# A gated graph network followed by graph attention, planned at build time: the order of the first layers, the last pair's second layer, and the plan's offsets

## The chip, the core and the metric

The kernel runs on one core of a Trainium2 chip. The engines named below are TensorE (PE; its weight loads are listed apart, as PEld), VectorE (DVE), ScalarE (ACT), GpSimd (POOL) and SyncE (SP), which issues the transfers. The time is the device time of one execution in microseconds, from its start to its end. One of the executions is recorded by the hardware profiler, and all rows of this document come from such a record.

## The reference

The input is 64 graphs of 256 nodes with 256 features, and an adjacency matrix for each with about 3% of its entries set. Two blocks follow one another, each with a layer norm, a relu and a residual. The first is three layers of a gated recurrent unit (GRU) over messages of the neighbours, the second one layer of graph attention.

```python
A = (adj != 0)
h = relu(layernorm(x))
for i in range(3):
    aggr = A.T @ (h @ weight[i])
    gi, gh = aggr @ w_ih.T + b_ih, h @ w_hh.T + b_hh
    r, z = sigmoid(i_r + h_r), sigmoid(i_z + h_z)
    n = tanh(i_n + r * h_n)
    h = (1 - z) * n + z * h
x = x + h
h = relu(layernorm(x)) @ W.T
e = leaky_relu(h @ a_left + (h @ a_right).T, 0.2)
x = x + softmax(where(adj == 0, -1e9, e)) @ h
```

`weight` differs from layer to layer, while `w_ih`, `w_hh` and the biases are shared.

## The kernel before

**Tiles.** Two graphs make a pair, and there are 32 pairs. A tile is 128 partitions by 512 elements: 128 features by the 2 x 256 nodes of a pair (the state `hT`, one tile for each of two blocks of features, 0 and 1), or 128 nodes by features in the other orientation. All tiles come from fixed classes: 28 `full` (f32), 22 `round` (TensorE's rounded f32), 40 `half` (16 bit), 8 PSUM banks, and a few more.

**Precision.** Matmuls take split operands. `split16` makes of a value its rounded head (name ending in `0`, on ScalarE), its remainder in 16 bits (`1`, on VectorE) and its whole in 16 bits (`d`). A gate is then one pass over heads (weights `fac_*`) and two over 16-bit parts (weights `low_*`), all accumulated in one bank (`gate`, L671, its matmuls at L668). The setup multiplies `weight[i]` by `w_ih` once (`G`, L595), so a layer computes its messages as `A.T @ h` and goes straight to the gates. `limbs` (L652) makes the head and the remainder, `hi` and `lo`, that the propagation takes.

**A layer of a pair** (in `pair`, L746) consists of: the splits of the state (`h0`, `h1`), the propagation `prop` on TensorE (L805), the splits of its result (`g0`, `g1`, from the bank), and for each block of features four gates: `r`, `nh` (own state, scaled at L690), `ni`, `z`. Behind them stand the sigmoid and tanh on ScalarE (L823, L833, L836) and five passes on VectorE: `u` L828, `u add` L831, `d sub` L840, `d mul` L842, `d add` L844. The new state is then turned back to the orientation that the next propagation needs. Pairs 1 to 30 do this by a transposing DMA (`dma_turn`, L700), gathers (L705) and a joining copy on ScalarE (`join`, L713). The first and the last pair do it on TensorE (`back`, L871). The last pair's last layer runs graph by graph, with 256 columns for each gate, and with its own back-transposes (L856). Two or more pairs are in work at a time.

**The attention** of a pair: norm and relu (L728 to L741), dot products on VectorE (L899), `right` (over DRAM, or by a transpose on TensorE in the last pair, L920), leaky relu (L925), mask (L928), max (L930), exponentials (L936; L1010 in the last pair), the transpose of the probabilities (by DMA, in the last pair on TensorE, L1018), `mix` (L965, L973, L1026) and `project` (L984, L995, L1034), the output (L1000, L1037) and its store (L1003). The last two pairs mix and project in plain f32 (L973, L995, L1026, L1034), the others with split operands.

**What sets the order.** Nothing is scheduled on the chip: each engine runs its queue in order. The queues are filled at build time by `Plan`, a list scheduler. Each operation has an engine, a time for which it occupies it and a time after which its result is there, all written as constants. Priorities are due times carried back along the dependences, less an offset from the table `LEAD`. That table is keyed by the operation's name, with a prefix for the first pair, the last (`last `) and the one before it (`late `); pairs without a prefix share one set of offsets, so the order repeats from pair to pair. Two things lie outside the priorities: `in_turn` makes the groups of gates (one for each layer of each pair) follow each other by a turn number, and `stage` holds a layer's entry back until an earlier group has begun. The turn number of layer i of pair p is 3p + 2i. So TensorE's gates run pair 0 layer 0, pair 0 layer 1, pair 1 layer 0, pair 0 layer 2, pair 1 layer 1, pair 2 layer 0 and so on: from there on one layer of another pair lies between two layers of a pair, but layers 0 and 1 of pair 0 are neighbours, and so are layers 1 and 2 of pair 31.

**The start.** `rows` (biases and attention vectors, L492 to L494) and the weights (`w load`, L511) are loaded, turned on TensorE (L522, L569), copied (L529) and split (`factor`, L545 to L552).

## Time and profile before

| | us |
|---|---|
| three runs | 1955.44, 1958.47, 1960.41 |
| median | 1958.47 |
| profiled execution | 1956.43 |
| its span, first to last instruction | 1954.6 |
| first TensorE instruction, from the span's start | 5.5 |

| work | busy us | instructions |
|---|---|---|
| matmuls of the gates (three groups of L668 by weights `low_hh`, `low`, `fac_hh`) | 621.7, 620.5, 433.4 | 2328, 2328, 1164 |
| joins on ScalarE, L713 | 342.5 | 304 |

A group's busy time is the sum over its instructions, its mean the time of one. TensorE's matmuls overlap in the record: the end of each is modelled and lies past the next one's start, so the spacing of two starts, not the duration, is what one costs. Idle time is shown with the instruction that ended it ("releaser"). The granted clock of TensorE is 0.998 of full speed on average; it is at half speed in a few stretches, the last ones of which begin at 1909.9 and 1940.6 us.

### The profile page before, as it was taken

The page shows a single profiled execution, that of the slowest core. Times are in us where ns is not written, and L with a number is a line of the kernel's source. Part 1 is how long each engine was busy: PE and PEld are TensorE (multiplying, and loading weights), DVE is VectorE, ACT ScalarE, POOL GpSimd, SP SyncE. Part 2 cuts the span into 40 slices and gives each one's busy share as a digit, 9 for nine tenths or more (in the row PEclk, how much of TensorE's full clock was granted, in tenths as well). Part 3 has the DMA queues.
Part 4 walks back from the last instruction along what each step waited for, and adds up shares of the span by engine and source line. Part 5 has one row for each costly group of instructions (what it writes and reads, how often), then busy time and mean ns, then how long its engine had stood idle before and what let it go on. Part 6 is the DMA issues. An engine that isn't in the chain of part 4 may idle for free.

```text
span 1954.6 us, 31416 instructions
## 1 busy us (share of the span) xinstructions
PE 1930.9 (99%) x10205; PEld 1198.8 (61%) x10205; DVE 1646.6 (84%) x3954; ACT 1609.6 (82%) x2773; POOL 199.4 (10%) x262
## 2 busy tenths in 40 slices
PE   8999999999999999999999999999999999999998
PEld 5566655666656666666656666666556566666667
DVE  7688888888898888888888888888888888898886
ACT  5578888888888888888889888888888888888875
POOL 2001011011011011111010110110110111110100
PEclk9999999999999999999999999999999999999999
DMA  4247876868776678966687766698766777666733
GB/s 123 48 78 144 137 135 123 115 122 138 141 135 121 116 130 137 143 123 119 121 138 141 135 122 117 120 142 139 127 122 113 140 136 139 123 118 121 122 76 60
DMA packets 734469, 239.43 MB, mean 122 GB/s; under 512 B 658256, under 2 KB 734304, under 8 KB 734304
## 3 DMA queue, kind: packets, MB, share of 16 engines
q1 hardware_dynamic: 734272, 237.41, 68.5%
q8 instruction: 80, 1.31, 0.3%
q14 instruction: 85, 0.70, 0.2%
q10 hardware_dynamic: 32, 0.01, 0.0%
HBM read 61.09 MB, written 16.84 MB: 40 GB/s over the span
## 4 chain that ended last, share of the span: by engine, by line
PE 82%; ACT 6%; DMA 5%; DVE 5%; issue 1%; SPq 1%; ACTq 0%; DVEq 0%
PE bank L668 66%; PE bank L805 7%; DMA full<-full 4%; PE bank L965 3%; PE bank L984 3%; ACT full L713 2%; ACT round L619 1%; SPq L705 1%; PE bank L595 1%; DVE half L625 1%; ACT half L630 1%; DVE full L828 1%; ACT round L654 1%; DVE full L1000 1%; ACT full L741 0%
## 5 line engine op out<-in xcount | busy, mean ns | idle before, releaser
L668 PE MATMUL bank<-half,low_hh 128*128 128x512 f16 (+1 forms) x2328 | 621.7, 378 | 5.3 <-DVE half L625 5.2
L668 PE MATMUL bank<-half,low 128*128 128x512 f16 (+1 forms) x2328 | 620.5, 378 | 1.2 <-DVE half L623 1.2
L668 PE MATMUL bank<-round,fac_hh 128*128 128x512 f32 (+1 forms) x1164 | 433.4, 454 | 0.0
L668 PEld LDWEIGHTS <-low_hh 128*128 128x128 f16 x2328 | 211.1, 98 | 271.5 <-issue 64.9
L713 ACT COPY full<-full 128x1024 uint16<-128x1024 uint16 x304 | 342.5, 1162 | 37.1 <-DMA full<-full 23.4
L668 PEld LDWEIGHTS <-low 128*128 128x128 f16 x2328 | 203.3, 98 | 275.4 <-issue 83.2
L668 PE MATMUL bank<-round,fac 128*128 128x512 f32 (+1 forms) x1164 | 367.1, 405 | 0.0
L668 PEld LDWEIGHTS bank<-round,fac 128*128 128x128 f32 x1164 | 217.5, 188 | 56.4
L668 PEld LDWEIGHTS bank<-round,fac_hh 128*128 128x128 f32 x1164 | 212.8, 189 | 62.9
L735 POOL TENSOR_TENSOR small<-small,nhalf 128x2 f32<-128x2 f32 x128 | 122.2, 955 | 1243.3 <-DVE small L733 1239.1
L833 ACT ACTIVATE full<-full,vec 128x512 f32<-128x512 f32 (+1 forms) x194 | 138.8, 717 | 83.3 <-DVE full L831 82.6
L836 ACT ACTIVATE full<-bank,b_rz 128x512 f32<-128x512 f32 (+1 forms) x194 | 131.3, 677 | 70.6 <-PE bank L668 68.7
L623 DVE TENSOR_TENSOR half<-bank,round 128x512 f16<-128x512 f32 x192 | 131.6, 687 | 59.8 <-ACT half L630 45.4
L625 DVE SCALAR_TENSOR_TENSOR half<-full,round 128x512 f16<-128x512 f32 x252 | 167.0, 682 | 2.4 <-ACT round L619 2.4
L655 DVE SCALAR_TENSOR_TENSOR half<-full,round 128x512 f16<-128x512 f32 x184 | 123.8, 688 | 46.4 <-ACT round L654 45.7
L690 ACT ACTIVATE bank<-bank,b_nh 128x512 f32<-128x512 f32 (+1 forms) x194 | 127.1, 655 | 40.7 <-PE bank L668 40.2
L823 ACT ACTIVATE full<-bank,b_rz 128x512 f32<-128x512 f32 (+1 forms) x194 | 131.7, 679 | 32.0 <-PE bank L668 25.9
L630 ACT ACTIVATE half<-bank 128x512 f16<-128x512 f32 x252 | 146.4, 597 | 11.7 <-PE bank L805 11.2
L619 ACT ACTIVATE round<-bank 128x512 fp32r<-128x512 f32 x252 | 146.8, 597 | 10.2 <-PE bank L805 9.2
L840 DVE TENSOR_TENSOR full<-full,full 128x512 f32<-128x512 f32 (+1 forms) x194 | 132.3, 682 | 25.9 <-ACT full L833 25.9
L619 ACT ACTIVATE round<-full 128x512 fp32r<-128x512 f32 x252 | 146.2, 629 | 2.2 <-DVE full L844 2.0
L842 DVE SCALAR_TENSOR_TENSOR full<-full,full 128x512 f32<-128x512 f32 (+1 forms) x194 | 132.1, 681 | 11.7 <-ACT full L836 10.3
(113 smaller groups left out, 2566.8 us busy)
## 6 DMA issues: line engine op xcount, KB each, us to landing
full<-full SPq DMA_DIRECT2D x484, 128.0 KB, 3.6
x<-in_x_dram SPq DMA_DIRECT2D x64, 256.0 KB, 3.1
adj<-in_adj_dram SPq DMA_DIRECT2D x64, 256.0 KB, 3.8
full<-in_x_dram SPq DMA_DIRECT2D x64, 256.0 KB, 3.7
full<-full SPq DMA_DIRECT2D x248, 64.0 KB, 3.3
out_dram<-full SPq DMA_DIRECT2D x62, 256.0 KB, 2.2
full<-line SPq DMA_DIRECT2D x62, 128.0 KB, 3.8
full<-full SPq DMA_TRANSPOSE x304, 3.4
```

What stands on the lines that cost most here:

```text
L619: act(name + " 0", A512 if bank else C512, lambda: nc.scalar.activation(v0.t, v.t, AF.Copy, scale=up), r=[(v, ALL)], w=[(v0, ONE)])
L623: rem = lambda: nc.vector.tensor_sub(v1.t, v.t, v0.t.bitcast(F32))
L625: rem = lambda: nc.vector.scalar_tensor_tensor(v1.t, v.t, up, v0.t.bitcast(F32), op0=ALU.mult, op1=ALU.subtract)
L630: act(name + " d", A512, lambda: nc.scalar.activation(vd.t, v.t, AF.Copy, scale=up), r=[(v, ALL)], w=[(vd, ONE)])
L668: return [(j, lambda start, j=j, kb=kb: nc.tensor.matmul(bank.t[:, cols], fs(j, kb), s[kb][j].t[:, cols], start=start, stop=True, skip_gro ...
L713: act(name, 1065, lambda: nc.scalar.copy(dst.t.bitcast(U16).rearrange("p (j n b) -> p j n b", j=2, b=2), src.t.bitcast(U16).rearrange(f"p ...
L805: nc.tensor.matmul(pa.t[:, ts(g, N)], b, m[:, ts(sb, N)], start=(n == 0), stop=True, skip_group_check=True)
L823: act(f"r {db}{of}", fit(575, part), lambda b=r_, k=pr, db=db, cols=cols: nc.scalar.activation(b.t[:, cols], k.t[:, cols], AF.Tanh, bias=b ...
L833: act(f"tanh {db}{of}", fit(615, part), lambda u=u, en=en, cols=cols: nc.scalar.activation(u.t[:, cols], u.t[:, cols], AF.Tanh, bias=b_i[: ...
L836: act(f"z {db}{of}", fit(575, part), lambda b=z_, k=pz, db=db, cols=cols: nc.scalar.activation(b.t[:, cols], k.t[:, cols], AF.Tanh, bias=b ...
L840: dve2(f"d sub {db}{of}", fit(V512, part), lambda u=u, d=d, cols=cols: nc.vector.tensor_sub(d.t[:, cols], d.t[:, cols], u.t[:, cols]), r=[ ...
L842: dve2(f"d mul {db}{of}", fit(V512, part), lambda d=d, b=z_, cols=cols: nc.vector.scalar_tensor_tensor(d.t[:, cols], b.t[:, cols], 1.0, d. ...
```

## The change

Four edits, and a new table of offsets.

1. The turn numbers come from a table `TURN`, in which layers 0 and 1 of pair 1 get the numbers 1 and 3. The order of the gates at the start becomes pair 0 layer 0, pair 1 layer 0, pair 0 layer 1, pair 1 layer 1, pair 0 layer 2, and goes on as before.
2. In the last pair, layer 1 runs graph by graph too (`apart` for i > 0): its gates, back-transposes and limbs. The entry of its layer 2 (splits of the state, propagation, splits of its result) runs graph by graph as well (`entry`). For this `split16` and `limbs` are rewritten to work on a part of the columns, and the gates read by parts. The pair has 320 operations in place of 272: 18 more on VectorE, 16 on ScalarE, 14 on TensorE. All other pairs have the operations they had.
3. In the plan, the result of `rows` is put at 5300 ns after its issue (3000 before), that of a weight load at 3900 (3434), with 500 ns of SyncE for each (600).
4. Pair 29 gets a prefix of its own, `pen `.
5. All offsets in `LEAD` are new, and so the order of all queues.

The remainder of the propagation's split, a subtraction before, becomes a `scalar_tensor_tensor` with a factor of 1.0.

```diff
...
-    "A": -93000, "A16": 28000, "G": -2000, "b_nh": 8000, "b_rz": -33500, "b_rz half": -33000, "back 0": -60500,
...
+    "A": -122000, "A16": -24000, "b_nh": 12000, "b_rz": -99500, "back 0": 113000, "back 0 gather": 5500,
...
+    "pen tanh 1": -40000, "pen total": -16000, "pen turn 0": 8000, "pen turn 0 gather": -9000, "pen turn 1": -16000,
...
-        plan.op("rows", "ACT", 200, 3000, load_rows, w=[(rw, ONE)])
+        plan.op("rows", "ACT", 200, 5300, load_rows, w=[(rw, ONE)])
...
-                dma("w load", 256, lambda b=b, r0=r0: nc.sync.dma_start(parts(b), view[:, r0 : r0 + 2, :]), w=[(b, ONE)])
+                plan.op("w load", "SP", 500, 3900, lambda b=b, r0=r0: nc.sync.dma_start(parts(b), view[:, r0 : r0 + 2, :]), w=[(b, ONE)])
...
-    def rounded(name, v, v0, up, bank=False):
-        act(name + " 0", A512 if bank else C512, lambda: nc.scalar.activation(v0.t, v.t, AF.Copy, scale=up), r=[(v, ALL)], w=[(v0, ONE)])
-    def remainder(name, v, v0, v1, up, dve_):
-        if up == 1.0:
-            rem = lambda: nc.vector.tensor_sub(v1.t, v.t, v0.t.bitcast(F32))
+    def split16(name, v, up, bank=False, part=None, whole=None, unit=C):
+        v0, v1, vd = whole or (Buf("round"), Buf("half"), Buf("half"))
+        cols, of = (slice(None), "") if part is None else (columns(part), " of %d" % part[0])
+        has = keys = ALL if part is None else part
+        cut = lambda ns: ns if part is None else fit(ns, part)
+        dve_ = dve if bank else dve2
+        act(f"{name} 0{of}", cut(A512 if bank else C512), lambda: nc.scalar.activation(
+            v0.t[:, cols], v.t[:, cols], AF.Copy, scale=up), r=[(v, has)], w=[(v0, keys)])
+        dve_(f"{name} 1{of}", cut(V512), lambda: nc.vector.scalar_tensor_tensor(
+            v1.t[:, cols], v.t[:, cols], up, v0.t[:, cols].bitcast(F32), op0=ALU.mult, op1=ALU.subtract), r=[(v, has), (v0, keys)], w=[(v1, keys)])
+        if bank:
+            act(f"{name} d{of}", cut(A512), lambda: nc.scalar.activation(
+                vd.t[:, cols], v.t[:, cols], AF.Copy, scale=up * unit), r=[(v, has)], w=[(vd, keys)])
         else:
-            rem = lambda: nc.vector.scalar_tensor_tensor(v1.t, v.t, up, v0.t.bitcast(F32), op0=ALU.mult, op1=ALU.subtract)
-        dve_(name + " 1", V512, rem, r=[(v, ALL), (v0, ONE)], w=[(v1, ONE)])
-    def whole_of(name, v, vd, up, bank):
-        if bank:
-            act(name + " d", A512, lambda: nc.scalar.activation(vd.t, v.t, AF.Copy, scale=up), r=[(v, ALL)], w=[(vd, ONE)])
-        else:
-            dve2(name + " d", 340, lambda: nc.vector.tensor_scalar(vd.t, v.t, up, None, op0=ALU.mult), r=[(v, ALL)], w=[(vd, ONE)])
-    def split16(name, v, up, bank=False, given=(None, None), part=None):
-        v0, v1 = given
-        vd = Buf("half")
-        if v0 is None:
-            v0 = Buf("round")
-            rounded(name, v, v0, up, bank)
-        if v1 is None:
-            v1 = Buf("half")
-            remainder(name, v, v0, v1, up, dve if bank else dve2)
-        whole_of(name, v, vd, up * (part or C), bank)
+            dve2(f"{name} d{of}", cut(340), lambda: nc.vector.tensor_scalar(
+                vd.t[:, cols], v.t[:, cols], up * unit, None, op0=ALU.mult), r=[(v, has)], w=[(vd, keys)])
         return v0, v1, vd
-    def turn16(name, src, cols, dst, place, n, **kw):
-        plan.op(name, "SP", T16, 4100, lambda: nc.sync.dma_start_transpose(
-            dst.t.bitcast(U16)[:, place].rearrange("p (c n) -> p c n", n=P), cols(src.t.bitcast(U16))), **kw)
-    def limbs(tag, v, b, c, dve_):
-        act(tag[0], C512, lambda: nc.scalar.activation(b.t, v.t, AF.Copy, scale=UP_V), r=[(v, ALL)], w=[(b, ONE)])
-        dve_(tag[1], V512, lambda: nc.vector.scalar_tensor_tensor(
-            c.t, v.t, UP_V, b.t.bitcast(F32), op0=ALU.mult, op1=ALU.subtract), r=[(v, ALL), (b, ONE)], w=[(c, ONE)])
+    def limbs(tag, v, b, c, dve_, part=None):
+        cols = slice(None) if part is None else columns(part)
+        src = lambda: v.t if part is None else v.t[:, :N]
+        keys = ALL if part is None else part
+        cut = lambda ns: ns if part is None else fit(ns, part)
+        act(tag[0], cut(C512), lambda: nc.scalar.activation(b.t[:, cols], src(), AF.Copy, scale=UP_V), r=[(v, ALL)], w=[(b, keys)])
+        dve_(tag[1], cut(V512), lambda: nc.vector.scalar_tensor_tensor(
+            c.t[:, cols], src(), UP_V, b.t[:, cols].bitcast(F32), op0=ALU.mult, op1=ALU.subtract), r=[(v, ALL), (b, keys)], w=[(c, keys)])
...
-                           r=[(s[kb][j], ALL) for _, s in ts_ for kb in range(DB) for j in range(3)] + [
+                           r=[(s[kb][j], part) for _, s in ts_ for kb in range(DB) for j in range(3)] + [
...
-        plan.prefix = {0: "first ", NPAIR - 2: "late ", NPAIR - 1: "last "}.get(p, "")
-        plan.stage = (3 * p, 2)
+        plan.prefix = {0: "first ", NPAIR - 3: "pen ", NPAIR - 2: "late ", NPAIR - 1: "last "}.get(p, "")
+        plan.stage = (TURN[p, 0], 2)
...
-            plan.stage = (3 * p + 2 * i, 1)
-            hs = [split16(f"h{db}", hT[db], UP_V, given=given[db]) for db in range(DB)]
-            given = [(None, None)] * DB
-            gs = []
-            for db in range(DB):
-                pa = Buf("bank")
-                def prop(db=db, pa=pa, hi=hi, lo=lo, first=i == 0):
-                    ops = [(hi, A), (lo, A16)]
-                    terms = [(part, a, g, sb) for part, a in (ops[::-1] if narrow[0] else ops) for g in range(G) for sb in range(NB)]
-                    for n, (part, a, g, sb) in enumerate(terms):
-                        if not first:
-                            b = part[db].t[:, ts(g * NB + sb, P)]
-                        elif part is lo:
-                            b = lo[g].t[:, ts(db * NB + sb, P)]
-                        else:
-                            b = blocks_of(part[g])[:, sb, db, :]
-                        m = a[g].t.bitcast(BF16) if part is lo else a[g].t
-                        nc.tensor.matmul(pa.t[:, ts(g, N)], b, m[:, ts(sb, N)], start=(n == 0), stop=True, skip_group_check=True)
-                pe(f"prop {db}", 4 * (PROP + PROP16), prop, r=[(b, ONE) for b in (hi + lo if i == 0 else [hi[db], lo[db]]) + A + A16], w=[(pa, ONE)], mixed=True)
-                gs.append(split16(f"g{db}", pa, 1.0, True))
+            plan.stage = (TURN[p, i], 1)
+            apart, entry = i > 0 and not far, [(0,), (1,)] if last and not far else [None]
+            triple = lambda: (Buf("round"), Buf("half"), Buf("half"))
+            hs, gs = [triple() for _ in range(DB)], [triple() for _ in range(DB)]
+            for part in entry:
+                for db in range(DB):
+                    split16(f"h{db}", hT[db], UP_V, part=part, whole=hs[db])
+            pas = [Buf("bank") for _ in range(DB)]
+            for part in entry:
+                for db in range(DB):
+                    def prop(db=db, pa=pas[db], hi=hi, lo=lo, first=i == 0, graphs=part or ALL):
+                        ops = [(hi, A), (lo, A16)]
+                        terms = [(part, a, g, sb) for part, a in (ops[::-1] if narrow[0] else ops) for g in graphs for sb in range(NB)]
+                        for n, (part, a, g, sb) in enumerate(terms):
+                            if not first:
+                                b = part[db].t[:, ts(g * NB + sb, P)]
+                            elif part is lo:
+                                b = lo[g].t[:, ts(db * NB + sb, P)]
+                            else:
+                                b = blocks_of(part[g])[:, sb, db, :]
+                            m = a[g].t.bitcast(BF16) if part is lo else a[g].t
+                            nc.tensor.matmul(pa.t[:, ts(g, N)], b, m[:, ts(sb, N)], start=(n == 0), stop=True, skip_group_check=True)
+                    of, graphs = ("", ALL) if part is None else (" of %d" % part[0], part)
+                    pe(f"prop {db}{of}", 2 * len(graphs) * (PROP + PROP16), prop, mixed=True, w=[(pas[db], graphs)],
+                       r=[(b, part or ALL) for b in (hi + lo if i == 0 else [hi[db], lo[db]])] + [(b[g], ONE) for b in (A, A16) for g in graphs])
+                    split16(f"g{db}", pas[db], 1.0, True, part=part, whole=gs[db])
...
-            tops = TOPS[3 * p + 2 * i] = []
-            apart = last and not far
+            tops = TOPS[TURN[p, i]] = []
             for part in [(0,), (1,)] if apart else [ALL]:
                 cols, of = columns(part), " of %d" % part[0] if apart else ""
                 for db in range(DB):
-                    plan.due = 1000.0 * SLOT * (3 * p + 2 * i) + (8000.0 * part[0] if apart else 0)
+                    plan.due = 1000.0 * SLOT * TURN[p, i] + (8000.0 * part[0] if apart else 0)
...
+                of = " of %d" % g
                 def back(g=g, db=db, hn=hn):
                     for k in range(NB):
                         nc.tensor.transpose(hn.t[:, ts(k, P)], hT[db].t[:, ts(g * NB + k, P)], ident)
                 pe(f"back {db} of {g}", 2 * TR, back, r=[(hT[db], (g,))], w=[(hn, ALL)])
-                dve(f"res {db} of {g}", 335, lambda g=g, db=db, b=XR[g], hn=hn: nc.vector.tensor_add(
+                if not last:
+                    limbs((f"hi {db}{of}", f"lo {db}{of}"), hn, hi[db], lo[db], dve, part=(g,))
+                    continue
+                dve(f"res {db}{of}", 335, lambda g=g, db=db, b=XR[g], hn=hn: nc.vector.tensor_add(
                     parts(b)[:, :, ts(db, P)], parts(b)[:, :, ts(db, P)], hn.t[:, :N].rearrange("p (k f) -> p k f", k=NB)),
                     r=[(hn, ALL)], w=[(XR[g], ALL)])
...
-                ps = split16(f"p{g}", pT, UP_P, part=1.0)
+                ps = split16(f"p{g}", pT, UP_P, unit=1.0)
...
     TOPS, SLOT = {}, 20
+    TURN = {(p, i): 3 * p + 2 * i for p in range(NPAIR) for i in range(L)}
+    TURN.update({(1, 0): 1, (1, 1): 3})
```

## The prediction

> **What bounds the kernel now.** I read the totals first, then TensorE's waits, then windows of the stages, then the chain of waits.
>
> ```profile
> span 1954.6 us, 31416 instructions
> PE 1930.9 (99%) x10205; PEld 1198.8 (61%) x10205; DVE 1646.6 (84%) x3954; ACT 1609.6 (82%) x2773; POOL 199.4 (10%) x262
> ```
>
> TensorE is busy 99% of the span. A reordering can only win what TensorE stands still, runs at a low clock, or spends before its first and after its last matmul. The waits show where it stands:
>
> ```profile
> PE bank L498 <- DMA rows<-in_L_gnn_b_hh_dram: 5.5, 1, 5.5
> PE bank L668 <- DVE half L625: 5.2, 10, 0.8
> PE bank L871 <- DVE full L844: 4.4, 4, 1.9
> PE bank L1018 <- ACT full L1010: 3.2, 1, 3.2
> PE bank L668 <- DVE half L623: 1.2, 2, 0.8
> PE bank L805 <- DVE half L655: 0.4, 1, 0.4
> ```
>
> Columns: us in total, times, longest. Of the 4.4 us at L871 (layer output turned back on TensorE) the timeline puts 0.21 and 1.87 us at 48.4 to 50.9 (pair 0, layer 0 to 1) and 1.41 and 0.88 us at 1906 to 1909 (pair 31, layer 1 to 2). L1018, 3.2 us, is in the last pair's attention. L625, L623 and L655 are short stalls spread over the steady part. Now the stages:
>
> ```profile
> 900.00:959.00 59.00, 59.00 (x314) 36.36 (x312) 51.12 (x124) 50.58 (x87) 6.39 (x8) 1.00 0.71 130
> ...
> 1900.00:1910.00 10.00, 7.71 (x40) 4.43 (x37) 9.58 (x33) 6.82 (x12) 1.04 (x2) 1.00 0.22 33
> 1910.00:1920.00 10.00, 9.99 (x75) 8.47 (x75) 6.50 (x13) 7.04 (x18) 0.00 (x0) 0.83 0.40 74
> 1920.00:1930.00 10.00, 9.98 (x89) 8.94 (x87) 6.69 (x19) 6.51 (x17) 0.00 (x0) 1.00 0.75 107
> 1930.00:1955.00 25.00, 17.82 (x96) 15.50 (x96) 13.51 (x50) 11.40 (x29) 1.38 (x2) 0.92 0.13 43
> ```
>
> Columns: busy us of PE, PEld, DVE, ACT, POOL, then granted clock. A steady pair has TensorE full; the end does not, and from 1910 to 1920 the clock is 0.83. A pair without a stall has a length that the chain of waits gives, by one recurring gate:
>
> ```profile
> 857.97 14.70 PE bank L668 x66
> ...
> 916.96 14.70 PE bank L668 x66
> ...
> 975.94 14.70 PE bank L668 x66
> ...
> 1036.71 14.70 PE bank L668 x66
> ```
>
> These starts lie 58.99, 58.98 and 60.77 us apart: a pair costs 58.985 us, and 1.79 us were lost in the last. From 264.69 to 1749.13 lie 25 pairs in 1484.4 us, 9.8 us over 25 x 58.985. For the whole steady part (70 to 1898 us) I take **10.8 us** lost: 13 waits with 6.8 us shown, and the rest because a modelled matmul end lies some 0.16 us behind the next possible start.
>
> **The change, part by part.** The spacing of TensorE's matmuls (start to start: 0.216 us for 512 f16 columns, 0.234 fp32r; 0.109 and 0.119 for 256) times their number gives 1909.4 us before and 1909.6 after. All else is stalls.
>
> *1. Pairs 0 and 1 alternate.* Before, layers 0 and 1 of pair 0 are adjacent, so 48.4 to 50.9 us stands bare: 2.08 us shown, **2.4** with the hidden share. After, layer 0 of pair 1, over 13 us of gates, stands there. It needs pair 1's adjacency, statistics, limbs and splits some 20 us earlier. That moves 5 to 6 us of VectorE work (eight passes of 0.69 or less, statistics 0.41 x2 and 0.15 x2 per graph) into 20 to 40 us, where VectorE is busy 10.00 of every 10 us and TensorE too. Factors of layers 2 and of W are put off for it, which frees about as much. Walking VectorE's new order from the first loads, pair 0's first own-state gate gets its operands about 1.2 us after TensorE could start it (0 to 2.5). Pair 1's transposed state (transposes, two gathers, join, two splits: 3.4 + 3.5 + 1.16 + 1.3 us and queueing, some 14.5 from about 35 us) is there at 48 to 49 against 51 needed. SP's first 19 transfers, weights, x and adjacency, keep their order, so pair 1's inputs land as before. Sum: -2.4 + 1.2 = **-1.2** (-3 to +1).
>
> *2. Landings in the plan.* `rows` and `w load` cost nothing; they only move orders. TensorE's first instruction waits for the first weight load (issued 0.74, landed 3.44 us) rather than for `rows` (5.3). But the next weights land at 5.7 to 9.8 us and pace it. I take **-0.3** (-1.5 to +0.5).
>
> *3. New leads, steady part.* 10 of 13 stalls are one wait: the first own-state gate (`nh 0`, layer 0) waits for `h1 1` (L625). In the old order that remainder sits on VectorE behind `d mul 0`, which hangs on a z gate only 2.67 us of TensorE work ahead: z on ScalarE 0.68, d mul 0.69, h1 1 0.69, and hand-overs 0.15 make 2.2, so any 0.5 us of queueing shows. Measured, that slack runs from +0.24 to -1.15 us by pair. In the new order the nearest gate it hangs on ended 6.68 us earlier and needs about 3.0. The way from SP (transpose 3.4, two gathers up to 5.4 when late) to its join keeps at least 8.9 us; before, one pass had 4.0. Against this, `lo 0` to layer 2's propagation has 2.67 us where it had 6.67, and needs about 1.5 (u add 0.69, lo 0.69). One wait per pair is eased, one made tight but not short. I take 2.5 of 10.8 left, **-8.3**. From neither side is it shown: nothing gained (0), or all but 0.8 gone (-10).
>
> *4. Last pair's layer 1 graph by graph.* 72 gate matmuls of 512 columns become 144 of 256; back-transposes, limbs, layer 2's propagation and splits are halved. Price on TensorE: 0.2 us, the difference of the sums above. [...]
>
> [...] The row from 1920 to 1930 is layer 2, which already runs 256 wide: PE 9.98 and PEld 8.94 us busy in the same 10 us, 89 matmuls, 0.112 us each. Loads lie beside matmuls. I follow the row: 0.2.
>
> [...] The trace has 0.50 from 1909.9 to 1913.3, so 1.7 us lost. [...] By the row the gain is 2.6 + 1.7 + 0.2 = 4.5.
>
> ScalarE and VectorE pay for the halves: 18 more instructions on VectorE, 16 on ScalarE (a half takes 0.42 to 0.50 us where a whole takes 0.66 to 0.72): so 18 x 0.2, under 4 us each, over some 25 us in which they are 65 to 95% busy. New distances: backs to propagation 1.35 to 2.2 us (needs 1.0), propagation to its gate 1.1 (needs 0.95 to 1.05). I put 0.6 of stall. Sum: +0.2 - 4.5 + 0.6 = **-3.7** (-5 to 0).
>
> *5. The end.* After the last gate (1929.85) 24.7 us pass, with 15.65 us of TensorE work in them. 3.4 us are the gap before L1018 (dots, leaky, mask, max, exps of a graph, which nothing covers), 1.5 a half clock behind it. The new order puts both `right` transposes behind the backs and keeps the late pair's and first graph's mix and project (6.9 us) for that gap. In return `right 0` comes when graph 0's dots may be 2 us short, and `d add 1` stands behind `res` on VectorE (about 1). From the last gate, the last graph's own chain takes 17 to 18 us, so up to 5 could go. I take **-2** (-5 to +1).
>
> The g remainder becomes another VectorE form: 0.687 against 0.682 to 0.691 us for that form, nothing.
>
> Sum: -1.2 - 0.3 - 8.3 - 3.7 - 2 = -15.5 from the profiled 1956.43, **1941**. That execution is 2.0 below the median 1958.47 of the three runs; set to the median it is **1942.5**.
>
> **Rivals.** 0.3%, 5.9 us, is what a measurement here can tell from no change.
>
> *A: the steady stalls only move.* Leads are one table for 28 pairs; `lo 0` or `hi 1` (4.0 us ahead, needs 2.1) could stand where `h1 1` stood. For: in both orders two layers of a pair are one layer apart, so the dependence is as tight. Against: measured distances above. Gain without term 3, 7.2: **1951**.
>
> *B: slower, by cover that is too thin.* In the new steady order `lo 0` of layer 2 hangs on a gate 2.67 us ahead. If VectorE has other work queued ahead of `u add` and `lo 0` (it is 87% busy, 51.12 of 59), each 0.69 us passes straight to TensorE, every pair, as the order is periodic. A new stall of s us per pair takes the place of the old 10.8: the kernel is slower by more than 0.3% once 28 s passes 10.8 + 7.2 (the other terms) + 5.9 = 23.9, so from s = 0.85, which means `lo 0` 0.85 + 1.17 of slack = 2.0 us late, three passes of VectorE in the queue. At 1.2 us a pair: 33.6 - 18.0 = 15.6 over the median, **1974**. Against: the old order's own thin place, 0.5 us of slack behind VectorE, lost only some 0.3 us a pair.
>
> *C: start and end give nothing.* Layer 1's halves only move the gap to ScalarE, the early part is bound by VectorE (10.00 of 10), term 3 stays: -8.3, **1950**.
>
> *D: all of it.* Every term at its better end, -3 - 1.5 - 10 - 5 - 5 = -24.5: **1934**.
>
> **How the numbers follow.** Forecast (terms within their ranges, 1937 to 1948) 0.62, A 0.13, C 0.12, D 0.08, B 0.05. The time is the forecast's, **1942.5**; 8 in 10 needs A's and C's nearer part and D: **1934 to 1953**. Faster by over 0.3% (below 1952.6): the forecast, D, most of A and C, 0.87; same 0.08; slower 0.05.
>
> **What would show it.** Step 1: no stall of TensorE near 48 us, none over 2 us before 70. Step 2: the first TensorE instruction before 5 us. Step 3: the L625 row gone or one or two left, no new row of some 28 waits; the gate above starting every 58.985 us; a new row with over 10 waits makes A or B true. [...] Step 5: less than 2 us idle at the attention's transposes, last gate to span end 22 to 23 us. The forecast is wrong if the pair length differs from 58.985 or the early stalls exceed 4 us.

## The result and the profile after

The changed kernel takes 1944.41 us (median of 4 runs, 1943.56 to 1945.35), the kernel before 1957.50 (median of 4, 1955.44 to 1960.41): a ratio of 0.9932, with a 95% interval from 0.9915 to 0.9949. The forecast was 1942.5. The profiled execution of the changed kernel took 1944.29 us, 12.1 less than that of before.

The totals and TensorE's waits of the changed kernel, in the columns shown above for the kernel before:

```profile
span 1942.5 us, 31422 instructions
...
PE 1928.4 (99%) x10277; PEld 1214.7 (63%) x10277; DVE 1650.2 (85%) x3972; ACT 1592.8 (82%) x2789; POOL 170.8 (9%) x262
```

```profile
PE bank L559 <- DMA full<-in_L_gnn_w_ih_dram: 3.6, 1, 3.6
PE bank L998 <- ACT round L662: 1.5, 1, 1.5
PE bank L1017 <- ACT round L662: 1.3, 1, 1.3
PE bank L694 <- DVE half L664: 1.0, 1, 1.0
PE bank L559 <- DMA full<-in_L_gnn_weight_dram: 1.0, 1, 1.0
PE bank L886 <- DVE full L873: 0.9, 1, 0.9
PE bank L886 <- ACT full L865: 0.7, 1, 0.7
```

(Lines have moved: gates L694, propagation L833, back-transposes L904 and, apart, L886, mix L998, project L1017, splits L662 to L667.) Three rows of before are gone: the back-transposes (4.4 us), the last pair's transposed probabilities (3.2), and the wait for the state's remainder (5.2 in ten waits). Two are new, one wait each, at `mix` and `project`, and the prediction has neither. The one wait left on L664 stands at 1765.20 us, at a matmul over `low`: there a propagation's remainder is late, not the state's. The windows of the end:

```profile
900.00:959.00 59.00, 59.00 (x314) 36.78 (x313) 49.90 (x121) 49.14 (x86) 4.36 (x7) 1.00 0.67 130
1890.00:1900.00 10.00, 10.00 (x92) 9.20 (x89) 9.72 (x36) 6.45 (x15) 1.55 (x2) 1.00 0.09 28
1900.00:1910.00 10.00, 9.86 (x86) 8.74 (x85) 9.58 (x35) 7.71 (x21) 0.00 (x0) 1.00 0.41 62
1910.00:1920.00 10.00, 9.68 (x83) 8.40 (x82) 9.34 (x28) 8.06 (x25) 0.69 (x1) 1.00 0.53 121
1920.00:1943.00 23.00, 17.58 (x104) 14.83 (x101) 13.36 (x45) 11.99 (x30) 1.08 (x1) 1.00 0.22 59
```

TensorE stays nearly full and at full clock through the last pair's last two layers, where before it had 7.71 of 10 us and a clock of 0.83. From 1890 to 1900 it does 92 matmuls in 10 us with 9.20 us of weight loads beside them: 0.109 us each at 256 columns. Between 300 and 1650 us a pair takes 59.03 us, nearly without exception; before, a pair without a stall took 58.99.

To see where the time went I keep one account for every record: TensorE's **loss** at a matmul is its start less the sum of the spacings, at full clock and without a stall, of all matmuls ahead of it. Between two points of the same work the loss grows by what TensorE stood still or ran slow. Stages are cut by the work done (60, 150, 192, 1862 us of matmul time, the last gate); the last column is the time from the last gate's start to the end.

| kernel | start to 60 | 60 to 192 | 192 to 1862 | to the last gate | last gate to end | span |
|---|---|---|---|---|---|---|
| before | 10.6 | 0.1 | 10.7 | 4.5 | 25.1 | 1954.6 |
| changed | 8.7 | 3.8 | 2.5 | 1.5 | 21.9 | 1942.5 |
| difference | -1.9 | +3.7 | -8.1 | -3.0 | -3.2 | -12.1 |

(The rest, 0.4 us, is matmul time that now lies ahead of the last gate.) Four gains, then, and one loss, of 3.7 us, between 60 and 192. Each row is one execution, and the first and last columns move with the clock from one execution to the next: the kernel before has its clock at half from 1940.6 to 1944.0, in the last column, the changed one has no such stretch before its last instruction.

### The profile page after: what moved, and what is told of

It reads as the page before. It is cut to its first block, busy times and chain, and to the rows that moved or that the text cites. A ratio compares the mean times of both kernels' runs of the same rounds, so it can differ in the third digit from the quotient of the medians.

```text
span 1942.5 us, 31422 instructions
## 1 busy us (share of the span) xinstructions
PE 1928.4 (99%) x10277; PEld 1214.7 (63%) x10277; DVE 1650.2 (85%) x3972; ACT 1592.8 (82%) x2789; POOL 170.8 (9%) x262
## 5 line engine op out<-in xcount | busy, mean ns | idle before, releaser
L694 PE MATMUL bank<-half,low_hh 128*128 128x512 f16 (+1 forms) x2352 | 622.9, 376 | 0.1
L694 PE MATMUL bank<-half,low 128*128 128x512 f16 (+1 forms) x2352 | 616.3, 376 | 1.0 <-DVE half L664 1.0
L694 PE MATMUL bank<-round,fac_hh 128*128 128x512 f32 (+1 forms) x1176 | 404.3, 437 | 0.0
L694 PE MATMUL bank<-round,fac 128*128 128x512 f32 (+1 forms) x1176 | 394.2, 426 | 0.1
L694 PEld LDWEIGHTS <-low 128*128 128x128 f16 x2352 | 216.2, 98 | 262.6 <-issue 44.8
L694 PEld LDWEIGHTS <-low_hh 128*128 128x128 f16 x2352 | 206.0, 98 | 259.9 <-issue 79.1
L694 PEld LDWEIGHTS bank<-round,fac_hh 128*128 128x128 f32 x1176 | 217.3, 189 | 62.5
L664 DVE SCALAR_TENSOR_TENSOR half<-bank,round 128x512 f16<-128x512 f32 (+1 forms) x254 | 171.5, 684 | 99.7 <-ACT round L662 84.0
L694 PEld LDWEIGHTS bank<-round,fac 128*128 128x128 f32 x1176 | 215.7, 189 | 57.9 <-ACT round L662 0.4
L761 POOL TENSOR_TENSOR small<-small,nhalf 128x2 f32<-128x2 f32 x128 | 99.9, 782 | 1709.8 <-DVE small L759 1705.6
L667 ACT ACTIVATE half<-bank 128x512 f16<-128x512 f32 (+1 forms) x254 | 150.9, 594 | 48.5 <-PE bank L998 28.4
L664 DVE SCALAR_TENSOR_TENSOR half<-full,round 128x512 f16<-128x512 f32 (+1 forms) x254 | 169.2, 679 | 4.9 <-ACT round L662 2.1
L857 DVE SCALAR_TENSOR_TENSOR full<-full,bank 128x512 f32<-128x512 f32 (+1 forms) x196 | 131.8, 673 | 40.9 <-ACT full L852 39.9
L662 ACT ACTIVATE round<-full 128x512 fp32r<-128x512 f32 (+1 forms) x254 | 152.6, 628 | 11.2 <-DVE full L873 10.0
L681 DVE SCALAR_TENSOR_TENSOR half<-full,round 128x512 f16<-128x512 f32 x184 | 126.3, 688 | 26.4 <-ACT round L680 26.3
L662 ACT ACTIVATE round<-bank 128x512 fp32r<-128x512 f32 (+1 forms) x254 | 144.1, 596 | 0.7 <-PE bank L833 0.5
```

What stands on the lines that cost most here:

```text
L662: act(f"{name} 0{of}", cut(A512 if bank else C512), lambda: nc.scalar.activation(v0.t[:, cols], v.t[:, cols], AF.Copy, scale=up), r=[(v, h ...
L664: dve_(f"{name} 1{of}", cut(V512), lambda: nc.vector.scalar_tensor_tensor(v1.t[:, cols], v.t[:, cols], up, v0.t[:, cols].bitcast(F32), op0 ...
L667: act(f"{name} d{of}", cut(A512), lambda: nc.scalar.activation(vd.t[:, cols], v.t[:, cols], AF.Copy, scale=up * unit), r=[(v, has)], w=[(v ...
L681: dve_(tag[1], cut(V512), lambda: nc.vector.scalar_tensor_tensor(c.t[:, cols], src(), UP_V, b.t[:, cols].bitcast(F32), op0=ALU.mult, op1=A ...
L694: return [(j, lambda start, j=j, kb=kb: nc.tensor.matmul(bank.t[:, cols], fs(j, kb), s[kb][j].t[:, cols], start=start, stop=True, skip_gro ...
L857: dve(f"u {db}{of}", fit(S512, part), lambda u=u, k=ph, b=r_, cols=cols: nc.vector.scalar_tensor_tensor(u.t[:, cols], b.t[:, cols], 1.0, k ...
```

## The experiments

The planner runs again for every edit of the kernel's text, so an edit can move more than what it names. Some kernels below therefore keep a planned order and move single instructions afterwards.

**The changed kernel again.** No edit.

> The changed kernel once more, unaltered. Its record has two stalls behind late transfers: 3.9 us of TensorE lost at 174 to 182 us, behind a transposing DMA issued at 153.5 us that landed after 8.1 us where 3.2 is the median, and about 1.1 us at 1760 to 1780. If the lateness is chance, the 3.9 us is missing here or stands elsewhere. If it comes from the order of transfers (two adjacency loads and an x load issued within 4 us around that transpose), it stands at the same place with the same size within 1 us. The four times known lie within 1.8 us of each other, which speaks for the second. Time either way 1943.5 to 1945.5.

1944.32 us (1942.65 to 1945.87). Loss from 60 to 192: 3.0 us, with the same waits at the same work (mix at 172.6, project at 178.5). So the place is not chance. SyncE's queue in the first record of the changed kernel (start, us that the issues took, line, kind):

```profile
151.41 1.99 SPq L512 DMA_DIRECT2D adj<-in_adj_dram  x2
153.50 1.27 SPq L726 DMA_TRANSPOSE full<-full  x1
154.81 0.58 SPq L512 DMA_DIRECT2D x<-in_x_dram  x1
155.50 0.42 SPq L944 DMA_DIRECT2D full<-line  x1
161.63 2.62 SPq L731 DMA_DIRECT2D full<-full  x4
164.35 2.65 SPq L726 DMA_TRANSPOSE full<-full  x2
```

The gathers (L731) wait for the transpose issued at 153.50, which landed only at 161.6, after 8.1 us (median of this kernel 3.2). Ahead of it stood two adjacency loads, landing at 158.6 and 160.5, after 7.2 and 7.6 us (median 4.5), so late themselves; why is open. While SyncE waits for that, all behind it waits too: at 164.35 it issues the transpose of pair 0's probabilities, and TensorE comes to them before they are ready:

```profile
174.50 0.73 PE L998 MATMUL bank<-round,round 128*128 128x256 f32 x4 [1.51 <-ACT round L662]
...
180.45 0.73 PE L1017 MATMUL bank<-fac_W,round 128*128 128x256 f32 x4 [1.26 <-ACT round L662]
```

**Two loads moved, and four.** In the planned order of the changed kernel, loads are moved down SyncE's queue: the two adjacency loads behind the first transpose of pair 0's probabilities, and in the second kernel also two residual loads of pair 28.

```diff
+        sp = [o for o in self.emitted if o.eng == "SP"]
+        for a, b in ((58, 64), (57, 64), (972, 974), (971, 974)):
...
+            self.later(sp[a], sp[b])
```

> The changed kernel, order kept, with two adjacency loads moved down SyncE's queue, from ahead of pair 3's input transpose (issued at about 152 us) to behind the first transpose of pair 0's probabilities. Nothing takes them before about 214 us. If they are what makes that transpose land after 7.5 to 8.1 us, it lands in under 5 us, SyncE is free to issue the probabilities' transpose some 3 us earlier, and TensorE's stalls at mix and project of pair 0 (3.1 to 3.9 us lost at 172 to 182 us) shrink to under 1: time 1940.5 to 1942. If the lateness has another cause, the loss stays above 2.5 us and the time within 1 us of the changed kernel.

> As the run with two loads moved, and also two residual x loads of pair 28 moved behind the two gathers that follow them on SyncE (issued at about 1744 us, one of those gathers landed after 6.0 to 6.5 us). If they cause the 1.0 to 1.3 us stall at 1765, it goes too: 1.2 us less than the run with two loads. If not, that stall stays.

1943.55 us (1942.37 to 1944.06) and 1940.62 (1939.47 to 1941.71). The transpose lands sooner. SyncE's queue with four loads moved (all lines 24 further down):

```profile
152.26 1.27 SPq L750 DMA_TRANSPOSE full<-full  x1
153.57 0.58 SPq L536 DMA_DIRECT2D x<-in_x_dram  x1
154.87 0.32 SPq L968 DMA_DIRECT2D full<-line  x1
157.06 2.63 SPq L755 DMA_DIRECT2D full<-full  x4
159.78 1.29 SPq L750 DMA_TRANSPOSE full<-full  x1
161.12 1.10 SPq L536 DMA_DIRECT2D adj<-in_adj_dram  x2
```

The gathers start at 157.06, 4.8 us behind the transpose and not 8.1 (5.7 with two loads moved), and the probabilities go at 159.78. Loss from 60 to 192 fell to 2.0 us with two loads moved and 1.4 with four, not under 1: the wait at project (1.5 and 1.0) stays, and its cause is open. So the two loads are about half of this loss.

In the medians two loads bought 0.9 us, less than the 2.4 to 3.9 forecast, and four 3.8, of which the two residual loads would be 2.9 where 1.2 was expected. The records do not bear that split out. The one with two loads moved has its clock at half from 1922.1 to 1925.5, far from any moved load:

```profile
1920.00:1930.00 10.00, 8.96 (x37) 7.31 (x38) 7.40 (x30) 6.60 (x14) 1.07 (x1) 0.83 0.10 16
```

It loses 1.2 us there (last gate to end 23.1, not 21.9). Moving the residual loads ended the stall at 1765, but another of 0.8 us came at 1638, so that the loss from 192 to 1862 is the changed kernel's. Of the 2.6 us by which the record with four loads moved is shorter than that of the changed kernel, 2.4 lie between 60 and 192; the rest of the 3.8 is not located. The kernel with four loads moved is the fastest of all here: a ratio of 0.9914 to before (0.9898 to 0.9930).

**Two VectorE instructions exchanged.** First by a dependence that the planner had to keep, in the kernel before and, reversed, in the changed one:

```diff
+        for p in range(2, NPAIR - 2):
+            split, mul = named[p, "" + "h1 1"][0], named[p - 1, "" + "d mul 0"][1]
+            plan.after(mul, split)
```

> The kernel before with one dependence added for pairs 2 to 29: on VectorE, h1 1 of a pair's layer 0 stands ahead of d mul 0 of the preceding pair's layer 1; offsets and all else as before. My theory (the ten L625 stalls come from h1 1 standing behind a pass that hangs on a gate only 2.67 us of TensorE work ahead): the L625 row of TensorE's waits goes, 5.2 us shown and some 7 with the hidden share; time 1950 to 1952.5 against 1957.5. Rival (h1 1 is late for another reason, a late gather or join ahead of it, so that order on VectorE does not matter): the row stays at 4 us or more and the time within 2 us of before. Second rival (the stall moves to the delayed d mul 0 and what follows it): L625 gone, another row of about the same sum, time unchanged.

> The changed kernel with the reverse dependence for pairs 2 to 29: h1 1 of layer 0 behind d mul 0 of the preceding pair's layer 1. In the changed order the z gate that d mul 0 hangs on ends 4.0 us of TensorE work ahead of the gate that takes h1 1, not 2.67; needs: z 0.68, d mul 0.69, out 0.48, h1 1 0.69 and hand-overs, 2.7 us. If distance is what decides, slack is about 1.3 us: no L664 row of over 2 us, time within 2 us of the changed kernel. If standing behind d mul 0 costs in itself, some 7 us come back: 1951.

2014.21 us (2012.16 to 2015.59) and 1962.76 (1960.90 to 1964.43): both far off. In the first the planner arranged the whole steady order anew (VectorE's order, which repeated after every pair, no longer repeats within five), so it does not test the exchange. It shows what another order can cost:

```profile
PE bank L965 <- DVE half L625: 12.1, 7, 2.4
PE bank L668 <- DVE half L623: 10.0, 8, 2.0
PE bank L984 <- DVE half L625: 7.9, 12, 3.2
PE bank L805 <- DVE half L655: 6.5, 11, 1.4
```

The old wait (state's remainder, L625 before a gate) is gone, and four others stand in its place, 36.5 us shown.

In the second kernel the steady order is that of the changed one, but for the moved pass: in a pair of the middle, VectorE's other 121 instructions and all those of ScalarE, TensorE and SyncE follow each other as they do there. There, from 320 to 1720 us of work, it loses only 1.4 us more than the changed kernel. Most of its 18.6 us lie elsewhere, where the planner did arrange anew: 2.8 from 192 to 320, 5.8 up to the last gate and 8.6 behind it. So its steady part agrees with the distance, and its time says nothing of it.

For a test free of such shifts the same was done again after planning: the exchange alone, all other instructions of all engines in their old order.

```diff
+        for p in range(2, 30):
+            self.later(named[p - 1, "d mul 0"][1] if p > 1 else None, named[p, "h1 1"][0])
```

> The kernel before, its planned order kept to the last instruction, with one exchange made after planning for 26 pairs (4 to 29): on VectorE h1 1 of layer 0 stands directly ahead of d mul 0 of the preceding pair's layer 1, not directly behind it. This is the test that the run with the added dependence was meant to be, and was not, since there the planner moved everything. My theory: the ten L625 stalls on TensorE are the wait for that d mul 0's gate. L625 row gone or under 0.5 us, no new row above 1 us, TensorE's loss from 200 to 1700 us down from 10.6 to about 4, time 1949.5 to 1952. Rival (h1 1 is late by its own inputs): row unchanged, time 1956 or more. Second rival (d mul 0, now 0.69 us later, hands the stall on to its layer's propagation): another row of the same sum, time 1956 or more.

> The changed kernel, order kept, with the reverse move after planning for 26 pairs (3 to 28): on VectorE h1 1 of layer 0 goes directly behind d mul 0 of the preceding pair's layer 1. Here that pass hangs on a gate that ends 4.0 us of TensorE work ahead of the taker, and needs z 0.68, d mul 0.69, h1 1 0.69, hand-overs 0.15, 2.2 us. If the distance in TensorE work decides, 1.8 us of slack stay: time within 1.5 us of the changed kernel, no new row. If standing behind d mul 0 costs in itself, 5 to 7 us come back: 1949.5 to 1951.5.

The exchange in the kernel before: 1954.48 us (1949.31 to 1958.50, 14 runs) against 1958.27, ratio 0.9978 (0.9968 to 0.9987). Its waits:

```profile
PE bank L693 <- DVE half L648: 1.9, 4, 0.8
PE bank L693 <- DVE half L650: 1.7, 4, 0.8
```

L650 is the old L625: from 5.2 us in ten waits to 1.7 in four. L648 (a propagation's remainder) went from 1.2 to 1.9. The loss from 192 to 1862 fell from 10.7 to 5.4 in the profiled execution, but that one is the fastest of the 14, 5.2 us under their median. The medians are the better measure: they moved by 3.8 us (by the interval 2.5 to 6.3) where 6 to 8.5 was expected. So the exchange explains about half of the steady gain of 8.1. The other half is not isolated; the new order differs in everything else too.

The reverse in the changed kernel, where the same pass hangs on a gate 4.0 us ahead: 1944.63 us (1944.21 to 1945.92), no change, steady loss 3.3 for 2.5. In 26 pairs the state's remainder is late twice, and briefly:

```profile
716.69 1.67 PE L719 MATMUL bank<-half,low_hh 128*128 128x512 f16 x7 [0.15 <-DVE half L689]
...
1543.73 1.46 PE L719 MATMUL bank<-half,low_hh 128*128 128x512 f16 x6 [0.42 <-DVE half L689]
```

So it isn't the place behind `d mul 0` as such that costs, but a place behind a gate that is too near.

**The new offsets alone, and the new structure alone.**

> The kernel before with the new table of offsets alone (old turns, last pair's layer 1 whole, old landings; names of the new halves and of pair 29's prefix find no operation and fall away). If the steady gain comes from the offsets alone: from 200 to 1700 us TensorE loses under 2 us (11 before, 1 in the changed kernel), so -8 there, the first 70 us lose 10 or more as before (bare gap at layer 0 to 1 of pair 0), the last pair about as before: 1948 to 1951. If the offsets only fit the new structure, the steady part gives nothing: 1956 or more.

> The changed kernel with the old table of offsets: new turns, last pair by graphs, new landings, old offsets (the new halves share the names that layer 2's halves had; pair 29's prefix finds none). If the steady gain is in the offsets, TensorE loses 9 to 12 us from 200 to 1700 us as before (1.0 in the changed kernel), while the start and the last pair keep some of their gain: 1951 to 1956. If structure carries it, the loss from 200 to 1700 us is under 4 and the time under 1949.

> The kernel before with the new turn numbers alone; old offsets, the planner runs again. My theory: no wait for L844 near 48 us, loss in the first 70 us from 10.6 down to 8.5 to 10; the steady stalls stay at 8 to 12 us as the order repeats as before: time 1954.5 to 1957. Rival (VectorE, busy 10.00 of 10 us from 20 to 40, is the bound and pair 1's work ahead of it costs as much as the gap): loss by 70 us 10.2 or more, no row near 48 but new ones before 45, time within 1 us of before or above.

| kernel | start to 60 | 60 to 192 | 192 to 1862 | to the last gate | last gate to end | median us |
|---|---|---|---|---|---|---|
| before + new offsets | 12.6 | 1.6 | 2.6 | 3.8 | 26.3 | 1951.95 (1948.77 to 1953.86) |
| changed + old offsets | 9.7 | 4.2 | 22.4 | 4.6 | 30.2 | 1977.86 (1977.08 to 1980.32) |
| before + new turns | 8.0 | 4.5 | 19.3 | 4.8 | 29.0 | 1974.45 (1971.47 to 1977.73) |

The new offsets bring the steady gain without any new structure (10.7 to 2.6), as expected; the time is 5.8 us below before and just above the 1948 to 1951 expected. With the old offsets, the new structure is 16 to 20 us slower than before. I had expected the steady part of these two to stay as it was. It doubled, though no pair but the first two and the last was touched. The records show why: in the kernels before and changed, VectorE's instructions repeat after 122, one pair; in these two they repeat only after 366, three pairs. A different beginning has led the planner into a different repeating order. The row that carries it with new turns alone:

```profile
PE bank L965 <- DVE half L623: 9.9, 9, 1.5
```

**One part of the change undone, new offsets kept.**

```diff
-    TURN.update({(1, 0): 1, (1, 1): 3})
```

```diff
-            apart, entry = i > 0 and not far, [(0,), (1,)] if last and not far else [None]
+            apart, entry = last and not far, [None]
```

> The changed kernel with the old turn numbers (3p + 2i throughout), all else as changed; the planner runs again. My theory: the gap at pair 0's turn from layer 0 to 1 is worth 2.4 us. It is back near 48 us as a wait for L873 of about 1.9 us, TensorE's loss in the first 70 us goes from 8.7 to 10.5 or 11.5, and with nothing else moved the time is 1946 to 1947.5. Rival: with pair 1's work no longer pulled ahead, VectorE is free and the start is as short as with the new turns: loss by 70 us under 9.2, time within 1 us of the changed kernel.

> The changed kernel with layer 1 of the last pair and the entry of its layer 2 whole again (512 columns), as before the change; new turns, landings and offsets kept; the planner runs again. My theory: the bare stretch between layers 1 and 2 of pair 31 comes back, two waits at L904 of 2 to 2.5 us in all and a stretch of 3.4 us at half clock behind them: TensorE's loss from 1890 us to the last gate goes from 1.5 to 4.5 or 6, time 1947 to 1949.5. Rival (the offsets alone cover that stretch): no granted clock under 1.00 there and a time within 1 us.

Without the turns: 1947.07 us (1946.46 to 1949.35). The start loses 12.3 instead of 8.7, and 60 to 192 only 0.8 instead of 3.8. So up to 192 the turns bought 0.6 us on balance, and what they won at the start they gave back behind it. All kernels with old turns lose 0.1 to 1.9 us from 60 to 192, all those with new turns and the planner's own order of loads 2.4 to 4.5, with old offsets too, where the waits stand elsewhere (propagation and gates at 165 to 192). The gap is back as expected, and costs more than its idle time. TensorE's timeline, then windows of 1 us:

```profile
48.23 0.66 PE L904 MATMUL bank<-ident,full 128*128 128x128 f32 x4
50.89 0.81 PE L904 MATMUL bank<-ident,full 128*128 128x128 f32 x4 [2.00 <-DVE full L873]
```

```profile
51.00:52.00 1.00, 1.00 (x7) 1.00 (x8) 1.00 (x3) 0.76 (x2) 0.00 (x0) 0.62 0.56 128
52.00:53.00 1.00, 1.00 (x6) 0.74 (x6) 1.00 (x2) 0.33 (x1) 0.00 (x0) 0.50 0.46 100
53.00:54.00 1.00, 1.00 (x5) 0.46 (x3) 0.06 (x1) 0.53 (x2) 0.00 (x0) 0.50 1.05 351
```

The clock is halved from 51.2 to 54.7: 1.7 us more. In the kernel before, the same gap (1.87 us idle) left no such mark:

```profile
51.00:52.00 1.00, 1.00 (x10) 0.95 (x11) 1.00 (x3) 0.92 (x2) 0.00 (x0) 1.00 0.37 83
```

With the last pair's layer 1 whole: 1952.00 us (1949.16 to 1955.30). That is 7.6 us more, over the 3 to 5 expected, and not at the expected place. The stage to the last gate lost 3.0 where 1.5 (not 4.5 to 6), its clock stayed at 1.00, and no wait for L904 appeared; the larger part, 6.1 us, is behind the last gate (28.0 for 21.9), where TensorE waits for the late pair's joins, and has half its clock from 1926.9 to 1930.3 (the first row's eight matmuls take 3.30 us):

```profile
1926.41 3.30 PE L1006 MATMUL bank<-full,full 128*128 128x256 f32 x8 [2.14 <-ACT full L739]
...
1934.32 0.92 PE L1006 MATMUL bank<-full,full 128*128 128x256 f32 x3 [1.67 <-ACT full L739]
```

Here the planner ran anew with offsets found for another structure, so these 7.6 us (9.0 in the record, 2.8 of them in the steady part) do not measure what the halves are worth; they probably exceed it.

## Why the prediction was right, and where it was not

The time lay 1.9 us above the forecast and within its range. That is closer than the parts: the profiled execution gained 12.1 us where 15.5 were summed up. And 15.5 from the median of 1958.47 is 1943.0, not the 1942.5 put down. The large term, the steady part, was right in kind and size; a cost of 3.7 us was missing, and smaller errors went the other way. Against the profiled execution, by the prediction's own steps:

| step | forecast | measured |
|---|---|---|
| 1 and 2, start | -1.5 | -1.9 |
| 3, steady part | -8.3 | -4.4 (-8.1 and +3.7) |
| 4, last pair by graphs | -3.7 | -3.0, less 0.4 of matmul time moved ahead |
| 5, end | -2 | -3.2 |

**Steps 1 and 2: right sum, two wrong parts.** The gap of 2.4 us went. The 1.2 us priced for a VectorE that is busy throughout did not come: VectorE is busy 9.55 and 9.66 of 10 us from 20 to 30 and 30 to 40, and TensorE has no wait there. In return the first weights won nothing: the first instruction comes at 3.6 us instead of 5.5, yet by 20 us the changed kernel has lost 0.5 us more than the kernel before. Some 1.2 us are waits for the next weight loads, as the prediction said. The rest it did not price: the transposes of the weights run at half speed, 0.21 us apart and not 0.11, until the first rise of the clock in the record, at 10.9 us; before, that rise comes at 8.7.

```profile
3.62 1.83 PE L559 MATMUL bank<-ident,full 128*128 128x128 f32 x6 [3.62 <-DMA full<-in_L_gnn_w_ih_dram]
6.41 1.11 PE L559 MATMUL bank<-ident,full 128*128 128x128 f32 x4 [0.96 <-DMA full<-in_L_gnn_weight_dram]
...
7.67 1.54 PE L606 MATMUL bank<-ident,full 128*128 128x128 f32 x6
```

This part varies with the moment of that rise: the same kernel's second record has it at 9.2 us, and a loss of 7.6 up to 60 us.

**Step 3: the mechanism right, one term missing.** From 192 to 1862 the loss fell by 8.1 us, to 2.5, as forecast. The ten waits for the state's remainder are gone, and the tests after planning show why, for about half of the sum: distance, in TensorE work, from the gate that the remainder's queue hangs on. A pair takes 59.03 us and not 58.99, 0.04 more, so this sign of being wrong did come, at 1.1 us for 28 pairs. (Of the prediction's sums, 13 waits with 0.16 us each on top of 6.8 come to 8.9, not 10.8; the account here has 10.7. And its 1909.4 us of work is some 10 us less than the account's; only the difference of 0.2 between the kernels was used.) What the step left out is the passage from the start to the repeating order. I had measured the covers in a steady pair ("keeps at least 8.9 us") and held SyncE's first 19 transfers for enough at the start. The alternation, step 1, moves pair 0's attention against pair 3's entry, and there two loads of 256 KB that nobody needs for 60 us stand ahead of a transpose that SyncE's whole queue waits for. Without the turns this stretch loses 0.8 us; with them and the two loads moved, 2.0. So the loads are about half of it, and the turns themselves the other half, by waits not followed further. That is 3.7 us I had not counted. They belong to the price of the turns, and they are the difference between the forecast of this step and its outcome.

**Step 4: right in sum, its cause only in part shown.** The waits at the back-transposes are gone and the clock is 1.00, so the old gap is priced by idle time and half clock together, as in the row, and not by idle time alone. But with layer 1 whole and the new offsets kept this stage lost 3.0 us, at full clock: there the offsets bring half of the gain without the halves. The stall of 0.6 put for the new short distances was 1.5. Of the 4.5 us of gain put down, 2.6 are the waits of 1.41 and 0.88 us with 0.16 hidden in each, and 1.7 the half clock from 1909.9 to 1913.3; no run shows the 0.2 added to them. The account has 4.5 lost in this stage before, and 1.5 after. The narrow matmuls cost what the row of before had said (0.112 us each): from 1890 to 1900 they lie 0.109 us apart, with 9.20 us of weight loads beside them.

**Step 5: low by 1.2.** The 3.2 us gap ahead of the transposed probabilities is gone, filled by the late pair's mix and project, and no gap of 2 us at `right 0` took its place; the waits left are 0.7 and 0.9 us at the last back-transposes. Part of the 3.2 is luck: in two other records of nearly the same end (two loads moved, reverse move) the clock was at half at these waits (in the first from 1922.1 to 1925.5), and the stage took 23.1 us and not 21.9. On the other side, the kernel with two instructions exchanged has the end of before without its half clock, and 24.1 us for 25.1. New offsets without the halves (26.3), or with layer 1 whole (28.0), gain nothing here.

Of the rivals, A and C did not occur. B did not occur in the changed kernel, but it is no invention: the planner's order for new turns with old offsets loses 19.3 us in the steady part, 9.9 of them shown in nine waits of that kind, at `mix` rather than at `lo 0`. They come once in every three pairs (at 350.9, 529.3, 708.7 us and so on), as that order repeats.

## What to carry to other kernels

Ask for each wait of the bounding engine which of its instructions the late operand's queue hangs on, and how much work lies between: a need of 2.2 us behind 2.67 us of work stalled ten times, behind 4.0 twice, by 0.4 us at most. Check that distance where the order changes its rhythm, too, and look at what stands ahead in an in-order queue that needs nothing yet: two loads moved a few places took 1.0 to 1.8 us out of one stretch. Count a gain where it arises and behind it: the turns won 3.6 us by 60 us and had lost 3.0 of them by 192. A table of offsets belongs to the structure that it was found for: the old one lost 16 to 20 us under the new turns, though the new one gained 5.8 under the old.

## What the runs showed of the hardware

**The clock.** In the record of before the granted clock rises at 8.68 us, falls at 1909.90, rises at 1913.32, falls at 1940.62, rises at 1944.04 and falls at 1954.28, past the last matmul. These times lie 557, 1, 8, 1 and 3 times 3.413 us apart. In the record of the changed kernel it rises at 10.88 and falls at 1942.82, past the last matmul too, 566 times 3.413 us later. Cut into stretches of that length, and with work counted by the spacings, the three stretches at whose end the clock fell in the record of before held 1.29, 0.38 and 0.24 us of work, so none of them was idle; the others at full clock held 1.65 us or more, those of the changed kernel up to its last matmul 1.39 or more.

The two kernels with the same gap differ in this as well. Without the turns the clock falls at 51.25 us, the 3.41 us ahead of it held 0.93 us of work, and the 3.4 us behind it are at half clock, which costs 1.7. In the kernel before, a stretch of the same cut ends in the middle of the gap, at 49.64; this one and the next held 2.2 us of work each, and the clock stayed at 1.00.

In the kernel before the clock rose at 8.68 us, when TensorE had done nothing but transposes since its first instruction at 5.45 (its first other matmul starts at 11.14). Of the work ahead of the fall at 1909.90, 1.29 us, some 0.9 are eight transposes.

**Transfers.** A transposing DMA behind two loads of 256 KB landed after 8.1 and 7.5 us in the two records of the changed kernel, and after 5.6 and 4.8 in the two where these loads were moved behind it (median in the first record 3.2).

**Spread.** The kernel before ranges from 1952.98 to 1963.40 us over 52 runs, the one with two instructions exchanged from 1949.31 to 1958.50 over 14, the changed one from 1942.65 to 1945.87 over 8. Part of it goes with the clock: the 13 runs of before with a mean of 0.997 have a median of 1960.55 us, the 15 with 0.999 one of 1956.56. A larger loss alone does not make a kernel vary: the changed kernel with the planned reverse dependence loses 8.1 us from 192 to 1862 and stays within 3.5 us over 12 runs.
